# Perceiver block on one core: padded context tails, x by tiles, and another order at the end of the linear attention

## The chip, the cores and the metric

The kernel runs on one core of a Trainium2 chip. The metric is device microseconds (us) of one execution; lower is better. The time before the change is 684.81 us, the median of three runs (684.4 to 684.9).

The engines go by short names here. PE is TensorE (matmuls), PEld its weight loads, DVE is VectorE, ACT is ScalarE, POOL is GpSimd, and SP (SyncE) issues nearly all of the transfers. A float32 matmul stands in the trace as two instructions.

## What is computed

There are 8 sequences of 64 tokens, so 512 rows of x with 512 features, and for each sequence 1601 rows of context. Three residual blocks follow one another:

```python
x = x + _L0_xattn_ref(_layernorm(x), ctx_1024, W, b)
#   trans_q = ctx @ W.T + b; softmax(p @ trans_q.T); relu(att @ ctx @ W.T + b)
x = x + _L0_attn_ref(_layernorm(x), wq, wk, wv, wo, proj, ...)
#   h = ln(x); q, k = elu((h @ w) @ proj) + 1 per head; causal linear attention:
#   out_s = q_s . sum(k v) / (q_s . sum(k) + 1e-6); x + out @ wo; then a gelu MLP
x = x + _L0_ffn_ref(_layernorm(x), w_router, w0, w1, wo)
#   mixture of 8 experts, each token goes to 2 of them
```

The linear attention has 16 heads of 64 features. 512 = 4 tiles of 128 rows, and a tile holds two sequences.

## The kernel before

All is float32. The order of the instructions on every engine is the order in which the kernel's text issues them, SP included; nothing reorders them.

**Cross-attention.** The context comes twice: by key in `ctxT` tiles, for the scores, and by row in `ctx` tiles, for the weighted sum. `stream` lists these transfers and the later weights in one order; `issue_to` issues them from SP as buffers of a ring of 12 come free (a tile is about 1 MB at most, and PE frees one by finishing its matmuls). For each tile t of two sequences, `key_group` computes scores against a quarter of the keys, `softmax` follows, `turn_scores` transposes the weights, and `weigh(t, g)` multiplies them with 512 context rows of each of the two sequences. 1601 rows are 3 groups of 512 and 65 more. These 65 are the tail: `tail[t]` holds them for both sequences of the tile, 65 partitions with 2 x 512 numbers each (260 KB), in a buffer of its own (L188), and `weigh(t, 2)` adds its product (L482) to the sum that L472 has built up. The tail of tile t stands in the stream behind the third group of context rows of that tile.

**The start.** x is loaded in two transfers of two tiles each (L99), then W (`w_sb`), then the first key tiles. The statistics of x (L335), its normalization (L346) and transposes (L358) lead to the projection of x (L368), which PE does before the first scores.

**Linear attention.** The heads are taken in pairs, in 8 steps j = 0 to 7. A step has four parts:
- `linear(j, which)`: the projection of all 512 rows to q or k of the two heads, eight matmul instructions each (L595).
- `features(j)`: eight matmul instructions with `proj` (L611), then on DVE two minima (`ex`, L622), on ACT two exponentials (L623), on DVE `phi` of q and of k (L626).
- `products(j)`: q times k by tiles on PE (`qk`, L635), then masked on DVE (`masked`, L640).
- `attend_j(j)`: the denominator `den` (L652) and the numerator `num` (L662) on PE from `masked`, then on DVE `rden` (L670), its reciprocal (L671) and `a_t` (L672).

In the loop a step's parts stand between the projections of the next steps. The last parts have no projections to stand between: after the loop come `attend_j(6)`, `features(7)`, and then `output(t, js)`, the product of `a_t` with `wo` (L691) for tile t and the steps js, put between what is left. `output(0, ...)` and `output(1, ...)` need only steps up to 5 at first, and take 6 and 7 afterwards. Behind that come the residual sum and layer norm of each tile (`join`, `normal`, `turn_h2`), and the MLP.

**Mixture of experts.** Tokens are routed and gathered, and the experts' weights stream through the same ring. This is the longer half of the kernel, from about 400 us on.

Of the kernel before, what the change touches and what calls it, by code (L numbers as in the profile page):

```python
# [21 lines left out]
B, S, D = 8, 64, 512  # L22
LK = 1601
NT = B * S // P
KC = D // P
GK = 512
NG = LK // GK
TAIL = LK - NG * GK
SW = -(-LK // 4)
WIDTHS = [min(SW, LK - SW * g) for g in range(4)]  # L30
H, DH = 16, 64
# [15 lines left out]
def perceiver_kernel(  # L47
# [22 lines left out]
    nc = tc.nc  # L70
# [14 lines left out]
    def acc_bank(name):  # L85
        return ps.tile([P, 512], F32, tag="acc", name=name)
# [8 lines left out]


    xs = resid.tile([P, NT, D], F32, name="xs")
    for t in range(0, NT, 2):
        nc.sync.dma_start(xs[:, t : t + 2, :], x[:, t : t + 2, :])  # L99
    moe = ctx.enter_context(tc.tile_pool(name="moe", bufs=1))  # L100
    mid = ctx.enter_context(ExitStack())
    xinp = mid.enter_context(tc.tile_pool(name="xinp", bufs=1))
# [16 lines left out]
    def stream(key, src):  # L119
        order.append((key, src))  # L120

    def stream_keys(t, g):
        if t < NT:
            for h in range(2):
                src = context_t[2 * t + h, D * SW * g : D * (SW * g + WIDTHS[g])]
                stream(("ctxT", t, g, h), src.rearrange("(p c k) -> p c k", p=P, c=KC))
# [45 lines left out]
    def in_ring(key):  # L172
        return key[0] not in places_of and key not in places_of and key[0] != "tail"

    def issue_to(n):

        while issued[0] < min(n, len(order)):
            key, src = order[issued[0]]
            if in_ring(key) and len(held) >= RING:
                if held[0] not in freed:  # L180
                    return
                held.pop(0)
            if key in places_of:
                t_ = places_of[key]
                nc.sync.dma_start(t_, src)
            elif key[0] == "tail":
                t_ = tails.tile([P, 2, D], F32, tag="tail", name="_".join(str(k) for k in key))
                nc.sync.dma_start(t_[:TAIL, :, :], src)  # L188
            else:
                width = WIDTHS[key[2]] if key[0] == "ctxT" else 512  # L190
                t_ = ring.tile([P, 4, width], F32, tag="ring", name="_".join(str(k) for k in key))
                nc.sync.dma_start(t_, src)
                held.append(key)
            streamed[key] = t_
            issued[0] += 1
# [5 lines left out]
    def need(*key):  # L201
        if key[0] not in ("ctxT", "ctx", "tail", "wv"):
            done(*[k for k in held if place[k] < place[key] - AHEAD + 1])
            issue_to(place[key] + 1 + AHEAD)
        else:
            issue_to(len(order))
        return streamed[key]
# [156 lines left out]
    def pw_half(half, hc):  # L364
# [10 lines left out]
        nc.scalar.copy(pw_t[:, hc, cols], bank[:, : 2 * P])  # L375

    issue_to(len(order))
    turn_p(0)
    turn_p(1)
# [32 lines left out]
    def key_group(t, g):  # L412
# [8 lines left out]
        for c in range(KC):  # L421
# [9 lines left out]
        nc.scalar.activation(  # L431
            all_scores[t][:, g * SW : g * SW + width], sc[:, :width], AF.Identity, bias=pb[:, t : t + 1]
        )
# [11 lines left out]
    def turn_scores(t):  # L445
# [5 lines left out]
        for g in range(NG + 1):  # L451
# [6 lines left out]
            else:  # L458
                nc.tensor.transpose(bank[:TAIL, :P], scores[:, NG * GK : LK], ident)
                nc.scalar.copy(e_t[:TAIL, 4 * NG, :], bank[:TAIL, :P])  # L460

    all_av, all_xo = {}, {}

    def weigh(t, g):
# [15 lines left out]
        if g == NG - 1:  # L480
            for h in range(2):
                nc.tensor.matmul(  # L482
                    av[h * S : (h + 1) * S, :],
                    e_t[:TAIL, 4 * NG, h * S : (h + 1) * S],
                    need("tail", t)[:TAIL, h, :],
                    start=False,
# [96 lines left out]
    if True:  # L583
        a_t = la1.tile([P, H * DH // P, B * S], F32, name="a_t")

        nj = H * DH // P
# [18 lines left out]
        def features(j):  # L605

            pr = {which: acc_bank(f"pr_{which}_{j}") for which in ("wq", "wk")}
            for r in range(2):
                rows = slice(r * DH, (r + 1) * DH)
                for which, other in (("wq", r), ("wk", 1 - r)):  # L610
                    nc.tensor.matmul(  # L611
                        pr[which][other * DH : (other + 1) * DH, :],
                        proj2[rows, :],
                        lin[which, j][rows, :],
                        start=True,
                        stop=True,
                    )

            ex = {}
            for which in pr:  # L620
                ex[which] = la2.tile([P, B * S], F32, tag="ex", name=f"ex_{which}_{j}")
                nc.vector.tensor_scalar_min(ex[which], pr[which], 0.0)  # L622
                nc.scalar.activation(ex[which], ex[which], AF.Exp)  # L623
            for which in pr:
                phi[which, j] = la2.tile([P, B * S], F32, tag=f"phi_{which}", bufs=1, name=f"phi_{which}_{j}")
                nc.vector.scalar_tensor_tensor(phi[which, j], pr[which], 0.0, ex[which], ALU.max, ALU.add)  # L626

        def products(j):

            banks_ = [mm_bank(f"qk_{j}_{r}") for r in range(2)]  # L630
            for t in range(NT):
                cols = slice(t * P, (t + 1) * P)
                for r in range(2):
                    rows = slice(r * DH, (r + 1) * DH)
                    nc.tensor.matmul(  # L635
                        banks_[r][:, cols], phi["wk", j][rows, cols], phi["wq", j][rows, cols], start=True, stop=True
                    )
            for r in range(2):
                m = masked[j, r] = la2.tile([P, NT, P], F32, tag="masked", name=f"masked_{j}_{r}")
                nc.vector.tensor_tensor(  # L640
                    m,
                    banks_[r].rearrange("p (t q) -> p t q", t=NT),
                    mask[:, None, :].to_broadcast([P, NT, P]),
                    ALU.mult,
                )

        def attend_j(j):


            den = acc_bank(f"den_{j}")  # L650
            for r in range(2):
                nc.tensor.matmul(  # L652
                    den[r * DH : (r + 1) * DH, :],
                    ones[:, :DH],
                    masked[j, r].rearrange("p t q -> p (t q)"),
                    start=True,
                    stop=True,
                )
            num = acc_bank(f"num_{j}")
            for t in range(NT):  # L660
                for r in range(2):
                    nc.tensor.matmul(  # L662
                        num[r * DH : (r + 1) * DH, t * P : (t + 1) * P],
                        v_sb[:, t, (2 * j + r) * DH : (2 * j + r + 1) * DH],
                        masked[j, r][:, t, :],
                        start=True,
                        stop=True,
                    )
            rden = la2.tile([P, B * S], F32, tag="rden", bufs=1, name=f"rden_{j}")
            nc.vector.tensor_scalar_add(rden, den, 1e-6)  # L670
            nc.vector.reciprocal(rden, rden)  # L671
            nc.vector.tensor_tensor(a_t[:, j, :], num, rden, ALU.mult)  # L672
# [14 lines left out]
        def output(t, js):  # L687
            if t not in wo_banks:
                wo_banks[t] = (mm_bank if t < 2 else acc_bank)(f"wo_{t}")
            for j in js:  # L690
                nc.tensor.matmul(  # L691
                    wo_banks[t],
                    a_t[:, j, t * P : (t + 1) * P],
                    wo_r[j // 4][:, j % 4, :],
                    start=(j == 0),
                    stop=(j == nj - 1),
                )

        attend_j(nj - 2)
        features(nj - 1)  # L700

        warm2 = small.tile([P, 1], F32, tag="warm2", name="warm2")
        nc.scalar.activation(warm2, eps, AF.Sqrt)
        output(0, range(nj - 2))
        products(nj - 1)
        output(1, range(nj - 2))
        attend_j(nj - 1)
# [704 lines left out]
```

## Time and profile before

| | |
|---|---|
| median of the runs | 684.81 us |
| profiled execution, its own time | 685.44 us |
| its span, first to last instruction | 683.7 us |
| mean granted clock of TensorE | 0.983 |
| PE busy | 638.9 us (93%) |
| PEld busy | 296.2 us (43%) |
| DVE busy | 179.1 us (26%) |
| ACT busy | 128.2 us (19%) |
| moved by DMA | 138.04 MB, mean 202 GB/s |
| transfers of ctx / ctxT / tail | 24 of 1024 KB / 32 of about 800 KB / 4 of 260 KB |

A row of the timeline or of a group reads: start and duration in us, the engine, the kernel's line, the operation, output <- inputs, shapes, count; in brackets, the idle time before it and what ended that. The rows of 40 slices give busy time in tenths for equal parts of the span. A busy PE isn't PE at its peak, since the ends of matmuls are modelled. Idle time of an engine that is not the bound costs nothing.

### The profile page before, as it was taken

To read this page: it belongs to the slowest core of one execution; us is meant where nothing else is said; L and a number is where in the kernel's file an instruction comes from. 1 tells how busy PE (TensorE), PEld (TensorE's weight loads), DVE (VectorE), ACT (ScalarE), POOL (GpSimd) and SP (SyncE) were. 2 spreads that over 40 slices of the span, in tenths; PEclk is the share of its full clock that TensorE was granted. 3 is DMA by queue.
4 is the path that set the end of the run, shared out by engine and by line. 5 is a ranking of instruction groups with operands and counts; after the bars stand their busy time and mean duration, and the time that the engine had idled before them with its cause. 6 is when DMAs were issued, how large, how long until landed. Compare 5 with 4: busy or idle time off the path is not lost. (4 is left out here: it accounts for less than half of the span.)

```text
span 683.7 us, 6217 instructions
## 1 busy us (share of the span) xinstructions
PE 638.9 (93%) x2376; PEld 296.2 (43%) x2376; DVE 179.1 (26%) x403; ACT 128.2 (19%) x240; POOL 61.7 (9%) x81
## 2 busy tenths in 40 slices
PE   4998989799999999999999998898999999989993
PEld 3643434244444444445444455543444344434441
DVE  4011323132228687670000035310311101110100
ACT  2241223220132121122011200211111111111110
POOL 2000000000000000041000002331012202120000
PEclk9999999999999999999999999699999999999998
DMA  8999999999601103021311323127397595694711
GB/s 328 418 420 385 418 385 413 370 367 422 232 13 62 62 0 124 1 69 55 112 62 73 106 79 126 61 61 265 136 390 257 199 357 175 233 348 175 283 17 18
DMA packets 24222, 138.04 MB, mean 202 GB/s; under 512 B 4164, under 2 KB 4164, under 8 KB 11896
## 3 DMA queue, kind: packets, MB, share of 16 engines
q1 hardware_dynamic: 20056, 129.90, 49.0%
q0 software_dynamic: 3024, 6.58, 4.3%
q10 hardware_dynamic: 1104, 1.07, 0.4%
q8 instruction: 23, 0.38, 0.2%
q14 instruction: 15, 0.12, 0.1%
HBM read 132.56 MB, written 4.97 MB: 201 GB/s over the span
## 5 line engine op out<-in xcount | busy, mean ns | idle before, releaser
L1081 PE MATMUL up<-e_up,xgT 128*128 128x512 f32 x224 | 100.2, 595 | 1.2 <-PEq L1310 1.2
L1081 PEld LDWEIGHTS up<-e_up,xgT 128*128 128x128 f32 x224 | 40.9, 190 | 50.4 <-issue 50.4
L1089 PE MATMUL y<-e_wo,hidT 128*128 128x512 f32 x128 | 61.0, 599 | 0.0
L792 PE MATMUL mlp<-w,hid_sb 128*128 128x512 f32 x128 | 58.8, 597 | 0.0
L1046 DVE TENSOR_TENSOR mid<-up,act 128x256 f32<-128x256 f32 x35 | 14.9, 425 | 164.2 <-ACT act L1044 159.7
L771 PE MATMUL hid<-v_sb,w 128*128 128x512 f32 (+2 forms) x144 | 56.6, 545 | 0.0
L472 PE MATMUL av<-ctx,eT 128*64 128x512 f32 x192 | 48.4, 617 | 7.3 <-DMA ctx<-in_ctx_dram 6.5
L423 PE MATMUL sc<-ctxT,pw_t 128*64 128x401 f32 (+1 forms) x256 | 48.1, 501 | 0.7 <-DMA ctxT<-in_ctx_T_dram 0.7
L771 PEld LDWEIGHTS hid<-v_sb,w 128*128 128x128 f32 x144 | 26.2, 190 | 29.1 <-issue 27.3
L792 PEld LDWEIGHTS mlp<-w,hid_sb 128*128 128x128 f32 x128 | 23.4, 190 | 24.9 <-issue 24.9
L1044 ACT ACTIVATE act<-up 128x256 f32<-128x256 f32 x35 | 13.4, 383 | 104.5 <-PE up L1081 95.7
L786 POOL TENSOR_TENSOR xin<-xin,b_bc 128x512 f32<-128x512 f32 x4 | 5.1, 1263 | 295.3 <-DVE rstd_h L728 291.1
L423 PEld LDWEIGHTS sc<-ctxT,pw_t 128*64 128x64 f32 x256 | 20.3, 136 | 26.3 <-issue 22.9
L1062 POOL DMA_INDIRECT out_dram<-y_sb,dst_late x11 | 16.8, 1529 | 161.1 <-ACTq L1310 103.7
L1089 PEld LDWEIGHTS y<-e_wo,hidT 128*128 128x128 f32 x128 | 22.4, 190 | 19.5 <-issue 19.1
L595 PE MATMUL wk<-h_t,wk 128*128 128x512 f32 x64 | 29.5, 604 | 0.0
L595 PE MATMUL wq<-h_t,wq 128*128 128x512 f32 x64 | 29.4, 602 | 0.0
L532 PE MATMUL v<-wv,h_t 128*128 128x512 f32 x64 | 28.7, 597 | 0.6 <-DVE h_t L519 0.6
L472 PEld LDWEIGHTS av<-ctx,eT 128*64 128x64 f32 x192 | 13.9, 140 | 35.3 <-issue 24.6
L691 PE MATMUL wo<-wo,a_t 128*128 128x512 f32 x64 | 28.6, 597 | 0.0
L671 DVE RECIPROCAL rden<-rden 128x512 f32<-128x512 f32 x8 | 26.8, 3354 | 0.3
L828 DVE TENSOR_TENSOR xs<-mlp,xs 128x512 f32<-128x512 f32 x4 | 2.8, 692 | 87.3 <-PE mlp L792 87.3
(230 smaller groups left out, 653.1 us busy)
## 6 DMA issues: line engine op xcount, KB each, us to landing
e_up<-in_L_ffn_up_dram SPq DMA_DIRECT2D x32, 1024.0 KB, 7.9
ctx<-in_ctx_dram SPq DMA_DIRECT2D x24, 1024.0 KB, 17.4
ctxT<-in_ctx_T_dram SPq DMA_DIRECT2D x24, 802.0 KB, 15.7
e_wo<-in_L_ffn_wo_dram SPq DMA_DIRECT2D x16, 1024.0 KB, 10.0
w<-in_L_attn_w_dram SPq DMA_DIRECT2D x8, 1024.0 KB, 11.7
ctxT<-in_ctx_T_dram SPq DMA_DIRECT2D x8, 796.0 KB, 16.7
big_up<-in_L_ffn_up_dram SPq DMA_DIRECT2D x4, 1024.0 KB, 7.9
wv<-in_L_attn_wv_dram SPq DMA_DIRECT2D x2, 1024.0 KB, 13.0
```

What stands on the lines that cost most here:

```text
L423: nc.tensor.matmul(sc[h * S : (h + 1) * S, :width], pw_t[:, c, (2 * t + h) * S : (2 * t + h + 1) * S], keys[h][:, c, :], start=(c == 0), s ...
L472: nc.tensor.matmul(av[h * S : (h + 1) * S, :], e_t[:, 4 * g + j, h * S : (h + 1) * S], rows[h][:, j, :], start=(g == 0 and j == 0), stop=F ...
L532: nc.tensor.matmul(bank, h_t[:, c, t * P : (t + 1) * P], wv_n[:, c, :], start=(c == 0), stop=(c == KC - 1))
L595: nc.tensor.matmul(bank, w[:, c, (j % 4) * P : (j % 4 + 1) * P], h_t[:, c, :], start=(c == 0), stop=(c == KC - 1),)
L671: nc.vector.reciprocal(rden, rden)
L691: nc.tensor.matmul(wo_banks[t], a_t[:, j, t * P : (t + 1) * P], wo_r[j // 4][:, j % 4, :], start=(j == 0), stop=(j == nj - 1),)
L771: nc.tensor.matmul(hid_banks[f][:, tokens], w[:, c, (f % 4) * P : (f % 4 + 1) * P], h2_t[:, c, tokens], start=(c == 0), stop=(c == KC - 1),)
L792: nc.tensor.matmul(acc[t], hid[:, t * P : (t + 1) * P], need("w2", f // 4)[:, f % 4, :], start=(f == 0), stop=(f == FF // P - 1),)
L1046: nc.vector.tensor_tensor(hid, bank[:, FQ:], act, ALU.mult)
L1062: nc.gpsimd.indirect_dma_start(out=out, out_offset=bass.IndirectOffsetOnAxis(ap=dst[:n, :], axis=0), in_=y_sb[:n, :], in_offset=None, boun ...
L1081: nc.tensor.matmul(bank, xg_t[:, c, :], up_of[q][:, c, :], start=(c == 0), stop=(c == KC - 1))
L1089: nc.tensor.matmul(y, h_t[:, j, :], w[:, 2 * (q % 2) + j, :], start=(q + j == 0), stop=(q + j == NQ))
```

## The change

It has three parts.

The tails are padded on the host from 65 rows to 80, the next multiple of 16, and the transfer brings all 80; the matmuls read 65 of them as before. x is loaded in four transfers of one tile each in place of two of two tiles. And after the loop of the linear attention, `features(7)` is issued ahead of `attend_j(6)`, and `output(0, 0..5)`, which stood in one piece behind both, is cut in two: steps 0 to 2 go ahead of `attend_j(6)`, steps 3 to 5 behind it.

```diff
+TAIL_ROWS = -(-TAIL // 16) * 16
...
-    for t in range(0, NT, 2):
-        nc.sync.dma_start(xs[:, t : t + 2, :], x[:, t : t + 2, :])
+    for t in range(NT):
+        nc.sync.dma_start(xs[:, t, :], x[:, t, :])
...
-                nc.sync.dma_start(t_[:TAIL, :, :], src)
+                nc.sync.dma_start(t_[:TAIL_ROWS, :, :], src)
...
-        attend_j(nj - 2)
         features(nj - 1)
 
         warm2 = small.tile([P, 1], F32, tag="warm2", name="warm2")
         nc.scalar.activation(warm2, eps, AF.Sqrt)
-        output(0, range(nj - 2))
+        output(0, range(0, 3))
+        attend_j(nj - 2)
+        output(0, range(3, nj - 2))
         products(nj - 1)
         output(1, range(nj - 2))
         attend_j(nj - 1)
...
     tail = _np.asarray(inputs["ctx_1024"])[:, NG * GK :, :]
-    inputs["ctx_tail"] = tail.reshape(NT, 2, TAIL, D).transpose(0, 2, 1, 3)
+    tail = _np.pad(tail, ((0, 0), (0, TAIL_ROWS - TAIL), (0, 0)))
+    inputs["ctx_tail"] = tail.reshape(NT, 2, TAIL_ROWS, D).transpose(0, 2, 1, 3)
```

## The prediction

> **What bounds the kernel now.** I read the slices of the span first, then the timeline of PE by stage, then the windows around its stalls, then the rows at the place of the edit. The slices (each 17.1 us):
>
> ```profile
> PE   4998989799999999999999998898999999989993
> ...
> PEclk9999999999999999999999999699999999999998
> DMA  8999999999601103021311323127397595694711
> ```
>
> PE is busy in nearly every slice. DMA is full in the first ten (to 171 us) and in no later one; there alone can a transfer set the pace. The clock's one digit below 9 inside the span stands for 427 to 444 us. In that first part PE waits long three times, each time for context rows:
>
> ```profile
> 61.92 4.92 PE L472 MATMUL av<-ctx,eT 128*64 128x512 f32 x13 [2.29 <-DMA ctx<-in_ctx_dram]
> ...
> 94.77 3.22 PE L472 MATMUL av<-ctx,eT 128*64 128x512 f32 x13 [1.47 <-DMA ctx<-in_ctx_dram]
> ...
> 129.58 3.22 PE L472 MATMUL av<-ctx,eT 128*64 128x512 f32 x13 [2.73 <-DMA ctx<-in_ctx_dram]
> ```
>
> After 129.58 no PE wait in this stage is for a transfer, so the landing before it sets the stage's end; PE time saved ahead of it is given back as longer waits. The stalls lie beside the tails. Windows (us, PE, PEld, DVE, ACT, POOL, clock, DMA share, GB/s):
>
> ```profile
> 44.00:58.00 14.00, 14.00 (x77) 5.98 (x76) 0.00 (x0) 2.86 (x6) 0.00 (x0) 1.00 1.02 420
> 58.00:63.00 5.00, 2.71 (x12) 0.83 (x11) 1.82 (x1) 2.20 (x3) 0.00 (x0) 0.98 1.02 301
> 63.00:90.50 27.50, 27.50 (x131) 11.74 (x129) 7.43 (x17) 5.48 (x12) 0.00 (x0) 0.94 1.02 420
> ...
> 125.00:130.50 5.50, 1.97 (x9) 0.54 (x10) 1.82 (x1) 3.60 (x4) 0.00 (x0) 1.00 1.02 276
> ```
>
> The stream runs at 420 GB/s and falls to 301 while the first tail's packets are under way; likewise to 299 (90.5 to 95.5), 276, and 268 (147.5 to 153.5). The engines stay busy (share 1.02): every packet takes longer. Beyond the tail's own bytes a dip loses 119*5/420 = 1.42 us of stream, then 1.44, 1.89 and 2.17.
>
> From 171 us on PE is the bound. The end of the linear attention on PE, then on DVE:
>
> ```profile
> 266.85 1.16 PE L635 MATMUL qk<-phi_wq,phi_wk 64*128 64x128 f32 x16
> 269.62 1.24 PE L652 MATMUL den<-masked,ones 128*64 128x512 f32 x3 [1.62 <-DVE masked L640]
> ...
> 273.12 5.42 PE L691 MATMUL wo<-wo,a_t 128*128 128x512 f32 x12
> 278.91 1.16 PE L635 MATMUL qk<-phi_wq,phi_wk 64*128 64x128 f32 x16 [0.37 <-DVE phi_wk L626]
> 280.00 5.42 PE L691 MATMUL wo<-wo,a_t 128*128 128x512 f32 x12
> 285.35 1.08 PE L652 MATMUL den<-masked,ones 128*64 128x512 f32 x4
> ```
>
> ```profile
> 264.82 3.35 DVE L671 RECIPROCAL rden<-rden 128x512 f32<-128x512 f32 x1
> ...
> 268.89 1.28 DVE L640 TENSOR_TENSOR masked<-qk,mask 128x512 f32<-128x512 f32 x2
> ...
> 272.06 3.35 DVE L671 RECIPROCAL rden<-rden 128x512 f32<-128x512 f32 x1
> ...
> 276.12 0.68 DVE L622 TENSOR_SCALAR ex_wq<-pr_wq 128x512 f32<-128x512 f32 x1
> ```
>
> PE finishes qk of step 6 near 267.9 but has to wait for masked, which stands on DVE behind step 5's reciprocal; then features 7's chain stands behind step 6's reciprocal, and qk of step 7 waits.
>
> **The order of the last steps.** Nothing is added or removed; features(7) moves ahead of attend_j(6), with half of output(0) between them. PE now takes 285.35 - 266.85 = 18.50 us from qk of step 6 to den of step 7. The same blocks without a wait, from starts of rows: qk 1.09 (278.91 to 280.00); features 1.02 (its first matmul is at 272.10, wo at 273.12); twelve wo matmuls 5.35 (280.00 to 285.35), of which 12*0.43 is spacing and 0.2 the switch to another kind, so six take 2.58 + 0.2 = 2.78; den and num 1.88 (285.35 to 287.23). The new order costs 1.09 + 1.02 + 2.78 + 1.88 + 2.78 + 1.09 + 5.35 = 15.99: **2.51 us less**. From the waits: 1.68 ahead of den, 0.60 inside that block (269.62 to 272.10 in place of 1.88) and 0.44 ahead of qk, less 0.2 for one switch more.
>
> Is it covered? Counting on the old clock, features end at 268.95, wo at 271.7, and masked is ready at 270.2: 1.5 us of cover. On DVE features 7 then follow masked at once: two minima, two phi at some 0.6 each with an exponential between them, as at 250.20 to 252.93, ready near 272.9; qk needs them at 276.4. DVE goes on with rden 6 (den ready at 272.8), its reciprocal (3.35) and a_t 6 to 277.7; masked 7 ends near 279.0, and attend 7 asks for it at 282.8. Queued behind the moved work are thus a_t 6 (read by wo after attend 7) and masked 7, both over 3 us early. Banks: features 7 take those of features 6, read by 264.2; attend 6 takes those of step 5, free at 268.97. ACT's exponentials come earlier, its table load stays behind them. No DMA is issued here, so no queue is passed. What is late next is a_t 7, as now: wo of step 7 waits 0.47 for it at 291.4, and all shifts together.
>
> Behind that, weight transfers wait for ring slots that PE frees and shift with it (no PE wait for a weight tile in the trace), so the gain reaches the end. One thing can bend it: from 428.1 to 441.7 the clock is at half in four steps of 3.41 us. A step more or less costs PE up to 1.7 us; which way a shift of 2.5 us turns it the trace can't say. I take 0 and keep 1.7 both ways.
>
> **x in four transfers.** Two issues more on SP, 0.4 us each (the two take 0.81 to 1.68), ahead of w_sb; 1 MB is then queued at 2.5 us, over 2 us of stream, so nothing runs dry. The first tile lands half a transfer earlier (512 KB at 420 GB/s are 1.25 us, so some 0.6), and its statistics start near 4.2 instead of 4.84. PE starts at most 0.6 earlier and gives it back at 61.92. Packets of 2 KB take 0.084 us where those of 4 KB take 0.159: 512*0.084 against 256*0.159 over 16 engines is 0.14 us of stream. SP lets eight transfers be open; two small ones ahead alter that only at the start. Taken at 0, between 0.6 less and 0.2 more.
>
> **Tails of 80 rows.** What is added is 15*4 KB per tail, 61 KB, 0.15 us at 420 GB/s; what may go is the dip. A tail's completion count rises in 14 steps where a transfer of 128 rows takes 16, so at most 14 engines carry its 65 packets, the busiest five or more. If 80 rows fill all 16, the busiest still carries five, and the first 65 rows stay where they are. The bounds: all that lies ahead of 129.5 of the dips vanishes, 1.42 + 1.44 + 1.5 = 4.4 us less (PE's three waits, 6.5 in all, can give that); or the dips grow with the rows, by 80/65, some 0.35 each, and the bytes 0.15: 2.8*0.5 = 1.4 more. Nearest row: x itself came in packets of 4 KB over 128 rows at 418 GB/s (4.5 to 5.0 us), so packet size isn't the cause, and covering 80 rows is nearer to 65 than to 128. I take 0.
>
> [...] No run here shows a tail of another height.
>
> **The sum.** 2.51 less + 0 + 0: the profiled execution, 685.44 (span 683.7), goes to 682.9. It lies 0.63 above the median of the runs, 684.81, so the forecast is 682.3.
>
> **The rivals.** *The dips go* (0.2): engines in step and no short engines' lead; for it, the dips grow from tail to tail (1.42 to 2.17) as the landings spread; against it, that the rows stay. Then 4.4 less besides: about 677.9. *The dips grow with the rows* (0.1): 1.4 back: about 683.7. *Slower* (0.08): three more engines, writing rows beyond 64 as well, draw the other transfers deeper into the slow-down, and the rate in a window falls from 300 to 200 GB/s: its 5*300 = 1500 KB then take 7.5 us, 2.5 more, 2.8 times ahead of 129.5 (the third tail's window lies ahead of it with 0.8), so 684.8 + 7.0 - 2.5 = 689.3. It decides from a rate below 234: 1500/234 is 1.4 us more per tail, 3.9 in all, the 2.5 given back and 1.4 more; for it speaks that in the dips packets of all engines, also those with other rows, take 1.5 to 2 times as long; against it, that the trace has so low a rate in one place alone, 181 GB/s at 12.5 to 13.0 us, beside the transfer of `xb_bc`. *The order doesn't pay* (0.07): DVE takes another order, or PE's waits move to phi 7; that leaves 684.8; the counted slack of 1.5 and 3.5 us speaks against it.
>
> **How the numbers follow.** The main case has 0.55, 682.3 with its own range 680.6 to 684.0 (the clock's 1.7 each way). The low end reaches to the case without dips, 678.0; the high end takes in the growth of the dips, 684.4. A measurement of this kernel tells about 0.2% (1.4 us) from no change: faster is under 683.4, 0.51 of the main case's 0.55, the 0.2 without dips and 0.05 of the third, 0.76; same 0.15; slower 0.09, the fourth case and a hundredth.
>
> **What would show it.** Right: den of step 6 with no wait for masked, qk of step 7 with none for phi, den of step 7 some 18.5 - 2.5 us after qk of step 6; the rate beside tails still near 300, ctx rows of the third pair landing near 129.5. Wrong: a rate near 420 beside the tails (far faster), or near 200 (slower); a new PE wait for a_t; more than four half-clock steps near 430.

## The result and the profile after

The changed kernel takes 686.38 us, the median of 14 runs (682.55 to 688.6); beside them the kernel before took 684.96 (14 runs, 684.4 to 686.98). The ratio is 1.001 [0.9998, 1.0023]: no gain, and within the 0.2% that the prediction called the same. The forecast was 682.3 with a range of 678.0 to 684.4. The profiled execution is the longest of the runs, 688.6 (span 686.9); a second one took 685.05, and where the two differ in what matters below, it is said.

The slices, to be held against those of before:

```profile
PE   4998989799999999999999999798999999989993
PEclk9998999999999999999999999699999999999998
DMA  8999999999420202011212223227497595694711
```

What was lost, was lost by 171 us: part of the transfers that came in the eleventh slice now come in the twelfth (4 and 2 where there were 6 and 0), and PE's clock has a second digit below 9, in the fourth slice (51 to 69 us). The linear attention itself did as forecast. PE's timeline there:

```profile
272.19 1.16 PE L636 MATMUL qk<-phi_wq,phi_wk 64*128 64x128 f32 x16
...
274.30 2.84 PE L692 MATMUL wo<-wo,a_t 128*128 128x512 f32 x6
277.08 1.08 PE L653 MATMUL den<-masked,ones 128*64 128x512 f32 x4
277.99 1.04 PE L663 MATMUL num<-masked,v_sb 128*64 128x128 f32 x16
278.96 2.84 PE L692 MATMUL wo<-wo,a_t 128*128 128x512 f32 x6
281.73 1.16 PE L636 MATMUL qk<-phi_wq,phi_wk 64*128 64x128 f32 x16
282.82 5.42 PE L692 MATMUL wo<-wo,a_t 128*128 128x512 f32 x12
288.17 1.08 PE L653 MATMUL den<-masked,ones 128*64 128x512 f32 x4
```

From qk of step 6 to den of step 7 it is 288.17 - 272.19 = 15.98 us. No bracket is left: neither den nor qk waits. But qk of step 6 starts at 272.19, where it was 266.85, so 5.3 us were lost before this place (3.3 in the second profile, 270.14).

Two places show where. First the start. Each row of a window gives its bounds and length, then PE, PEld, DVE, ACT and POOL, then clock, DMA share and GB/s. Before:

```profile
3.50:5.00 1.50, 0.00 (x0) 0.00 (x0) 0.16 (x1) 0.00 (x0) 1.28 (x8) 1.00 0.93 333
5.00:6.50 1.50, 0.00 (x0) 0.00 (x0) 1.43 (x5) 0.29 (x1) 0.75 (x1) 1.00 1.10 431
```

After:

```profile
3.50:5.00 1.50, 0.00 (x0) 0.00 (x0) 0.73 (x2) 0.00 (x0) 1.28 (x8) 1.00 0.91 224
5.00:6.50 1.50, 0.00 (x0) 0.00 (x0) 1.27 (x5) 0.54 (x2) 0.75 (x1) 1.00 0.97 244
```

DVE begins earlier, as forecast, but the bytes come at 224 and 244 GB/s where they came at 333 and 431. By the last packets of each transfer, x is complete at 8.81 (6.49 before) and `w_sb` at 11.33 (8.98 before), 2.35 us late; SP's wait for the first key tile behind it ends at 13.31 where it ended at 11.11. In the second profile `w_sb` is complete at 9.81. PE's rows of the first projection and of the three long waits:

```profile
11.46 5.25 PE L369 MATMUL pw<-h_t,w_sb 128*128 128x256 f32 x16 [2.00 <-DMA w_sb<-in_L_xattn_W_dram]
...
63.39 2.83 PE L473 MATMUL av<-ctx,eT 128*64 128x512 f32 x6 [2.60 <-DMA ctx<-in_ctx_dram]
...
98.19 2.37 PE L473 MATMUL av<-ctx,eT 128*64 128x512 f32 x10 [2.23 <-DMA ctx<-in_ctx_dram]
...
133.23 3.73 PE L473 MATMUL av<-ctx,eT 128*64 128x512 f32 x10 [2.71 <-DMA ctx<-in_ctx_dram]
```

The wait for `w_sb` is new. The third long wait ends at 133.23 where it ended at 129.58 (at 129.91 in the second profile). Second, the windows of tail and clock in the profile after:

```profile
44.00:58.00 14.00, 13.76 (x75) 6.57 (x75) 0.00 (x0) 2.86 (x6) 0.00 (x0) 1.00 1.02 419
58.00:65.00 7.00, 4.05 (x14) 1.04 (x12) 1.82 (x1) 2.32 (x3) 0.00 (x0) 0.82 1.02 300
...
62.00:70.00 8.00, 6.61 (x18) 2.01 (x20) 0.00 (x0) 1.64 (x2) 0.00 (x0) 0.57 1.02 384
134.00:138.00 4.00, 4.00 (x14) 1.13 (x11) 0.00 (x0) 0.00 (x0) 0.00 (x0) 0.57 1.01 418
```

The dip beside the first tail is there as before: 300 GB/s against 419. Stream time lost beside the four tails, from packets, is 2.00, 2.17, 2.82 and 1.64 us (before, worked out alike: 1.41, 1.51, 2.22, 2.21). Of the third, some 0.8 us was lost from 118 to 124 us, ahead of that tail's packets (128.2 to 133.3). What has grown is the half clock at the end of the waits: from 62.4 to 69.2 (before: 62.8 to 66.2) and from 134.1 to 137.5 (before: not at all). In the second profile it is at half from 129.1 to 135.9 alone. The steps are 3.41 us each, with a granted clock of 0.50, and in them matmul instructions of 512 columns start 0.85 us apart, at the full clock 0.43: half the work, so 1.7 us less in a step.

### The profile page after: what moved, and what is told of

It reads as the page before. It is cut to its first block, busy times and chain, and to the rows that moved or that the text cites. A ratio compares the mean times of both kernels' runs of the same rounds, so it can differ in the third digit from the quotient of the medians.

```text
span 686.9 us, 6217 instructions
## 1 busy us (share of the span) xinstructions
PE 641.2 (93%) x2376; PEld 296.7 (43%) x2376; DVE 179.7 (26%) x403; ACT 128.2 (19%) x240; POOL 61.4 (9%) x81
## 5 line engine op out<-in xcount | busy, mean ns | idle before, releaser
L473 PE MATMUL av<-ctx,eT 128*64 128x512 f32 x192 | 51.9, 649 | 9.0 <-DMA ctx<-in_ctx_dram 9.0
L473 PEld LDWEIGHTS av<-ctx,eT 128*64 128x64 f32 x192 | 15.4, 146 | 39.0 <-issue 25.7
```

Of the source, the lines that this page charges most:

```text
L473: nc.tensor.matmul(av[h * S : (h + 1) * S, :], e_t[:, 4 * g + j, h * S : (h + 1) * S], rows[h][:, j, :], start=(g == 0 and j == 0), stop=F ...
```

## The experiments

Ratios are to the kernel before, run beside each, with a 95% interval; 0.1% is 0.69 us.

**The three parts alone, and the order with tails of 128 rows.** Before: 685.49.

The order alone:

```diff
-        attend_j(nj - 2)
         features(nj - 1)
...
-        output(0, range(nj - 2))
+        output(0, range(0, 3))
+        attend_j(nj - 2)
+        output(0, range(3, nj - 2))
```

> The kernel before with the new order of the last steps alone. Theory A (the prediction's: the order gains 2.5 us, x and the tails cost nothing) and theory B (the order gains 2.5, and x and the tails give it back in the transfer-bound first stage) both expect 2.5 us less than before, 682.4, and 15.99 us from qk of step 6 to den of step 7 in the profile. Rival C (the order's gain does not reach the end, as routing or the clock take it back) expects within 0.7 us of before with the same 15.99 us in place.

683.68 us, ratio 0.9971 [0.9960, 0.9981], so 2.0 us less (1.3 to 2.7): the order pays, and the 2.5 that its rows say lie within the interval.

x in four alone:

```diff
-    for t in range(0, NT, 2):
-        nc.sync.dma_start(xs[:, t : t + 2, :], x[:, t : t + 2, :])
+    for t in range(NT):
+        nc.sync.dma_start(xs[:, t, :], x[:, t, :])
```

> The kernel before with x in four transfers alone. Theory A expects no difference (within 0.5 us), the wait ahead of the third pair of context rows taking up what the start gains or loses. Theory B expects 1 to 2.4 us more, w_sb landing near 11 us instead of 8.98, and the context rows of the third pair landing that much behind 129.5. Rival C: no difference.

688.16 us, 1.0039 [1.0024, 1.0054]: 2.7 us more, for an edit taken at nothing. The second half of x is where it slows; `w_sb` is complete at 11.23:

```profile
3.50:5.00 1.50, 0.00 (x0) 0.00 (x0) 0.74 (x2) 0.00 (x0) 1.28 (x8) 1.00 0.60 150
```

At 150 GB/s the 16 engines are busy 60% of the time only, though `w_sb` is already queued behind. This is the lowest of the profiles: five others with x in four like this have 224 to 268 GB/s there, at a share of 0.76 to 0.91.

Tails of 80 rows alone:

```diff
+TAIL_ROWS = 80
...
-                nc.sync.dma_start(t_[:TAIL, :, :], src)
+                nc.sync.dma_start(t_[:TAIL_ROWS, :, :], src)
```

> The kernel before with tails of 80 rows alone. Theory A expects no difference (within 0.5 us) and rates beside the tails near 300 GB/s as before. Theory B expects 1 to 1.4 us more, the windows of low rate growing by 80/65 in length or depth. That the missing engines caused the low rate would give some 4 us less and 420 GB/s beside the tails.

686.10 us, 1.0007 [0.9997, 1.0016]: 0.5 us more, or nothing. The three together, -2.0 + 2.7 + 0.5 = 1.2, agree with the whole change's +0.7 (-0.1 to +1.6).

The new order with tails padded to a whole tile, and x in two transfers as before:

```diff
+TAIL_ROWS = 128
```

> The new order, and tails of 128 rows (63 of them zeros), with x in two transfers. Three readings of the low rate beside the tails: if it comes from a transfer that covers only part of the 128 partitions, 128 rows show 420 GB/s throughout; a tail then costs 0.6 us for 252 KB more and saves 1.4 to 2.2, net some 2 us less ahead of the third pair, so 680 with the order's 2.5. If it comes from the number of packets of 4 KB, the low rate lasts twice as long and the time is some 4 us above e1_order. If a tail's cost is bytes alone, 1.7 us above e1_order.

678.92 us, 0.9901 [0.9886, 0.9916], 4.8 us less than the order alone: the best version of all, ahead of both kernels, though each tail moves nearly twice the bytes. The windows beside its first and third tail, and its clock at the place of the third wait:

```profile
57.00:62.00 5.00, 3.64 (x19) 1.42 (x17) 1.82 (x1) 1.66 (x2) 0.00 (x0) 1.00 1.02 416
...
122.00:128.00 6.00, 3.83 (x18) 1.01 (x16) 1.82 (x1) 3.60 (x4) 0.00 (x0) 1.00 1.02 419
```

The dip is gone: 0.05, 0.06, 0.10 and 0.03 us of stream lost. PE's waits shrink, and the stage ends earlier (the first projection of the linear attention starts at 180.4, with the order alone at 184.7):

```profile
60.49 3.22 PE L473 MATMUL av<-ctx,eT 128*64 128x512 f32 x13 [1.36 <-DMA ctx<-in_ctx_dram]
...
92.36 3.22 PE L473 MATMUL av<-ctx,eT 128*64 128x512 f32 x13 [0.80 <-DMA ctx<-in_ctx_dram]
...
125.76 3.22 PE L473 MATMUL av<-ctx,eT 128*64 128x512 f32 x13 [1.35 <-DMA ctx<-in_ctx_dram]
```

Its profile has no half clock before 421 us, where that of the order alone has one step (129.0 to 132.4). How much of the 4.8 us is the stream and how much the clock wasn't measured apart.

**Which heights keep the dip.** Before: 686.28. Both have the new order and x in two transfers. One brings 64 of the tail's 65 rows:

```diff
+TAIL_ROWS = 64
...
-                    e_t[:TAIL, 4 * NG, h * S : (h + 1) * S],
-                    need("tail", t)[:TAIL, h, :],
+                    e_t[:TAIL_ROWS, 4 * NG, h * S : (h + 1) * S],
+                    need("tail", t)[:TAIL_ROWS, h, :],
```

The other pads them to 112:

```diff
+TAIL_ROWS = 112
```

> The new order, and tails of 64 rows: the last key of each sequence is left out of the weighted sum, so the time alone is to be read. 64 rows are four packets for each of 16 engines. If low rates come from covering half of the partitions, they stay near 300 GB/s beside the tails and the time is within 0.7 us of e1_order (683.7). If they come from five packets per engine, or from a row count that is no power of two, they go, and the time is some 4 us below e1_order, 679 to 680.

> The new order, and tails of 112 rows (7 packets on each of 16 engines). If the low rate shrinks as more of the partitions are covered, the loss beside a tail lies between those of 80 rows (1.4 us and more) and of 128 (none): 680 to 682. If only a full 128 rows avoid it, the loss is as with 80 rows or more, some 1 us above e1_order.

The packets on each engine in the two expectations are an estimate, rows over 16; no record tells the engines apart. 64 rows: 686.25, 0.9999 [0.9989, 1.0008]. 112 rows: 686.05, 0.9997 [0.9988, 1.0007]. Both are about 2 us worse than the order with 65 rows, more than either expectation had. Their profiles have half clock behind the waits from 95.0 to 101.8 and 132.5 to 135.9 (64 rows) and from 128.4 to 135.2 (112), one or two steps more than the order alone, which may be the 2 us; no run separates it. The windows of 64 rows:

```profile
58.00:63.00 5.00, 3.26 (x16) 1.04 (x14) 1.82 (x1) 2.17 (x3) 0.00 (x0) 1.00 1.03 307
92.00:97.00 5.00, 2.11 (x6) 0.53 (x6) 1.82 (x1) 3.60 (x4) 0.00 (x0) 0.79 0.97 257
```

and of 112:

```profile
92.00:97.00 5.00, 2.82 (x12) 0.77 (x12) 1.82 (x1) 3.60 (x4) 0.00 (x0) 1.00 1.01 308
126.00:132.00 6.00, 2.58 (x6) 0.72 (x8) 1.82 (x1) 3.13 (x4) 0.00 (x0) 0.70 1.01 272
```

So the loss isn't in proportion to the rows left out. 112 rows have 343 GB/s beside the first tail and lose 0.96, 1.74, 2.38 and 2.44 us beside the four tails, much like 65 or 80, and 128 rows lose none. A loss that shrinks with the rows missing is refuted; why only the full height escapes isn't settled (see the last section).

**How x is cut.** In the same comparison, four transfers from a tensor laid out tile by tile on the host (256 KB in one piece each):

```diff
-    for t in range(0, NT, 2):
-        nc.sync.dma_start(xs[:, t : t + 2, :], x[:, t : t + 2, :])
+    for t in range(NT):
+        nc.sync.dma_start(xs[:, t, :], x[t])
```

> Four transfers of x as in e2_x4, but x laid out tile by tile, so that each transfer reads 256 KB that lie together instead of 2 KB out of every 8 KB. If the loss of e2_x4 (2.7 us) comes from reading with that step, it goes: within 0.7 us of before, w_sb landing near 9 us. If it comes from packets of 2 KB or from two issues more, it stays: 2 to 2.7 us above before, w_sb near 11.

and x in one transfer:

```diff
-    for t in range(0, NT, 2):
-        nc.sync.dma_start(xs[:, t : t + 2, :], x[:, t : t + 2, :])
+    nc.sync.dma_start(xs, x)
```

> x in one transfer of 8 KB rows, one issue fewer than before. If the start of the transfers sets the first stage, larger pieces gain a little, 0 to 1 us, w_sb landing near 8.5, though the first statistics start at 5.5 to 6 us instead of 4.84. If PE's start sets it, 0.5 to 1 us more.

Tile by tile: 687.00, 1.0012 [1.0003, 1.0022]. One transfer: 685.83, 1.0001 [0.9989, 1.0012]. Tile by tile, 0.8 us (0.2 to 1.5) of the 2.7 are left, so most of the cost goes with the 2 KB pieces that lie 8 KB apart, and the rest with four transfers as such. The same windows of the start, tile by tile:

```profile
3.50:5.00 1.50, 0.00 (x0) 0.00 (x0) 1.43 (x3) 0.29 (x1) 1.28 (x8) 1.00 0.91 259
5.00:6.50 1.50, 0.32 (x2) 0.35 (x3) 1.43 (x5) 0.29 (x1) 0.76 (x1) 1.00 1.17 440
```

and in one transfer:

```profile
3.50:5.00 1.50, 0.00 (x0) 0.00 (x0) 0.00 (x0) 0.00 (x0) 1.28 (x8) 1.00 0.98 410
5.00:6.50 1.50, 0.00 (x0) 0.00 (x0) 0.66 (x1) 0.00 (x0) 0.77 (x1) 1.00 1.01 421
```

One transfer has `w_sb` complete at 8.31, earlier than before (8.98), and gains nothing: its first statistics start later (5.84), and the stage's end is set elsewhere. Tile by tile, all of x is there at 6.15, earlier than before (6.49), yet `w_sb` only at 10.26 and not near 9. SP issues `w_sb` at 1.27 with one transfer of x, at 1.74 with two and at 2.69 with four: in these three profiles the landing shifts with the issue and by more than it, so about half of the 2.35 us of the change seems to come from the two issues more.

Then, before: 685.95, four transfers again, with x padded so that the pieces of 2 KB lie 10 KB apart:

```diff
-        nc.sync.dma_start(xs[:, t : t + 2, :], x[:, t : t + 2, :])
+        nc.sync.dma_start(xs[:, t, :], x[:, t, :])
...
+    inputs["x"] = _np.pad(x_rows, ((0, 0), (0, 1), (0, 0)))
```

> Four transfers of x as in e2_x4, with x padded in memory so that the 2 KB pieces lie 10 KB apart instead of 8 KB. If the power-of-two step is what makes their reading slow, most of the loss goes, as in e5_x4_together: within 1 us of before, all of x landed by 6.5 us. If any scattered pieces of 2 KB are slow, it stays: 2 to 2.7 us above before, the last tile of x landing near 8.8 us and w_sb near 11.

687.22, 1.0024 [1.0013, 1.0035], x complete at 7.55 and `w_sb` at 10.15. The time lies between that of the pieces 8 KB apart and that of tile by tile, with intervals that overlap both ways. How much of the cost is the distance of the pieces and how much their size isn't settled.

**x with the dips gone.** In the same comparison, the order and 128 rows with x in one and in four transfers:

> The new order, tails of 128 rows, x in one transfer. With the low rates gone the first stage still waits for transfers (PE waited 1.9, 1.4 and 1.9 us in e4_order_tail128), so a landing of w_sb earlier by 0.7 us, as in e6_x1, may come through whole: 678.2, or nothing if the slower engine of the sixteen sets the landing: 678.9.

> As e4_order_tail128, with x in four transfers as in the change. If the late start of the stream passes through the transfer-bound stage to the end, 2 to 2.7 us above e4_order_tail128: 681 to 681.6. If it cost time only by making the low rates beside the tails worse, nothing: 678.9.

679.51, 0.9909 [0.9890, 0.9928], and 678.89, 0.9913 [0.9890, 0.9937]. With x in two it was 0.9901 [0.9886, 0.9916]. Here x in four costs no 2.7 us that can be seen, though in its profile the first projection of the linear attention still starts 1.5 us later (181.9 against 180.4). The intervals reach 1.3 and 1.6 us to either side, so about that much may be hidden. Neither profile has half clock before 421 us. (PE's waits with x in two were 1.36, 0.80 and 1.35 us by the rows above, shorter than the first expectation has them.)

**What the late stream does to the clock.** The parts alone left this open: with x in four the third wait ends at 130.02, only 0.4 us after before's, yet the linear attention starts 3.1 us later (187.4 against 184.3). Between them lies a half clock that before's profile doesn't have. The row behind the wait shows it: 5.93 us for 13 matmuls that took 3.22 before.

```profile
130.02 5.93 PE L472 MATMUL av<-ctx,eT 128*64 128x512 f32 x13 [2.65 <-DMA ctx<-in_ctx_dram]
```

Windows of 15 us around that wait; before:

```profile
125.00:140.00 15.00, 11.46 (x38) 4.50 (x38) 3.33 (x4) 4.18 (x5) 0.00 (x0) 1.00 1.02 369
```

x in four alone:

```profile
125.00:140.00 15.00, 11.57 (x31) 3.57 (x28) 2.57 (x2) 3.60 (x4) 0.00 (x0) 0.77 1.02 379
```

PE is busy as long (11.57 against 11.46), but with 31 matmuls in the records instead of 38. To test it, three matmuls whose result is never read go ahead of the third group of context rows of tiles 0 to 2, where PE would wait; into the change, into x in four, and into the kernel before (before: 686.18):

```diff
+        if g == NG - 1 and t < 3:
+            idle = mm_bank(f"idle_{t}")
+            for c in range(3):
+                nc.tensor.matmul(idle, pw_t[:, c, :P], pw_t[:, c, :], start=(c == 0), stop=(c == 2))
```

> The changed kernel with three idle matmuls (2.6 us, result unused) on PE ahead of the third context group of tiles 0 to 2, where it waits 2.8 to 3.4 us for rows. They fit into the wait. Theory D (much of the loss is PE running at half clock for 3.4 to 6.8 us after a wait of over 2.5 us) expects no half-clock stretch between 60 and 140 us and 1.5 to 3 us less than the change, 683.4 to 685. Theory B (the loss is the later landing of rows alone) expects no gain: 686.4 or up to 1 us more.

> e2_x4 with the same idle matmuls. Theory D: 1.5 to 3.4 us less than e2_x4 (its profile has two half-clock stretches behind the third wait), 685 to 686.5, so that x in four transfers costs about 1 us of late stream. Theory B: as e2_x4, 688.

> The kernel before with the same idle matmuls. Its profile has a half-clock stretch at 62.8 only, ahead of a later wait, so theory D expects 0 to 1 us less (runs of before that fall into a stretch near 130 gain), theory B 0 to 0.5 more.

The change with it: 683.60, 0.9967 [0.9954, 0.9980], 2.8 us below the change without. x in four: 685.43, 1.0005 [0.9992, 1.0017] (without: 1.0039). The kernel before: 684.11, 0.9982 [0.9969, 0.9996], so it had some of this loss itself. In the change's timeline the idle work fills the wait:

```profile
126.55 2.84 PE L474 MATMUL idle<-pw_t 128*128 128x512 f32 x6
129.33 1.07 PE L477 MATMUL av<-ctx,eT 128*64 128x512 f32 x2
131.30 3.22 PE L477 MATMUL av<-ctx,eT 128*64 128x512 f32 x13 [0.90 <-DMA ctx<-in_ctx_dram]
```

The window of 15 us around it has the full clock:

```profile
125.00:140.00 15.00, 14.10 (x49) 5.23 (x46) 2.66 (x3) 4.12 (x5) 0.00 (x0) 1.00 1.02 374
```

In none of the three is the clock at half anywhere before 426 us. So the half clock behind the waits is shown to cost, and keeping PE busy takes it away.

**When the clock falls.** The late stream isn't needed for it: the order alone, with x in two, has a step at half from 129.0 to 132.4 too. In each of the 17 profiles kept, all changes of the clock are whole multiples of 3.41 us apart, on a grid that lies elsewhere in each. Cut by that grid, the profiles have 3194 windows at full clock. PE was busy for at most 1.51 us in 49 of them, and after each of these the next window was at half; with 1.52 or 1.53 us it was so after two of four, and with 1.57 or more after none. A window at half was followed by full clock only where PE was busy for 3.02 us or more of it. So it is not a wait's length alone that decides, but how it falls on the grid. The longest wait of the kernel before, 2.73 us ahead of 129.58, is cut by it into two windows with 1.78 and 1.52 us of work, and costs no half clock; the change's, 2.71 us, leaves one window of 0.86 us (130.68 to 134.09).

## Why the prediction was wrong

The forecast gain didn't come: two steps failed, and a third was on the mark.

- **The order of the last steps: right.** 15.99 us were forecast for the stretch and 15.98 are there, without the waits that were to go. Alone it brought 2.0 (1.3 to 2.7) of the 2.51, and the stage behind it kept the gain: from the first projection of the linear attention to the first of the MLP it is 308.6 - 189.6 = 119.0 us, before 305.8 - 184.3 = 121.5. The rival "the order doesn't pay" is refuted.
- **x in four transfers: the step that failed.** It was taken at 0, at most 0.2 more, from "512*0.084 against 256*0.159" and "nothing runs dry". The sum takes the engines to be full. It measured +2.7 alone (1.6 to 3.7): the engines fell to a share of 0.60 and 150 GB/s with work still queued (0.91 and 224 GB/s in the change's profile), and about half of the delay of `w_sb` seems to come from the two issues that "nothing runs dry" was to cover. The earlier start of the statistics (forecast near 4.2) did come, and was worth nothing, since the projection then waited 2.00 us for `w_sb`, which the prediction had behind it in the queue but did not follow.
- **The clock: the step that was missing.** The prediction kept 1.7 us both ways for the half clock near 430 alone. The row that it showed for 63 to 90.5, with a clock of 0.94, already held a half step behind the first wait, and it was read past. Later transfers lengthen PE's waits for context rows (9.0 us in all where it was 6.5; 7.6 in the second profile), and behind some of them PE runs at half for one or two steps of 3.41 us. Behind the third wait nothing gives that back. With the waits filled, the change stands at 0.9967 and the kernel before at 0.9982, so 1.0 us better; without, 0.7 worse. By these medians the half clock costs the change 1.7 us more than it costs the kernel before, but each of the three ratios has an interval of about 0.9 us to either side. x in four then costs 1.6 still (1.0005 against 0.9982). That fits the late stream: in the profiles with the waits filled, the linear attention starts at 184.96 with x in four and at 182.93 without.
- **Tails of 80 rows: right, with half the reason.** Taken at 0 and measured at +0.5 (-0.2 to +1.1), inside its bounds of -4.4 and +1.4. "The dips go" did not come with 80 rows, and "covering 80 rows is nearer to 65 than to 128" held. But nearness is the wrong idea: 112 rows are no better (308 and 272 GB/s in the windows above, against 416 and 419 with 128). The price named for that rival was nearly the truth for 128 rows: 4.8 measured, 4.4 forecast, in part by luck if some of the 4.8 is the clock's.
- **The slower rival: refuted as a mechanism.** It had dips deepened by the rows beyond 64, with a rate below 234 GB/s and 7.0 us to pay. With 80 rows alone the four tails lose 1.64, 1.83, 2.26 and 2.30 us of stream, before 1.41, 1.51, 2.22 and 2.21: 0.7 us more in all. That isn't clear of the scatter: from 3 us ahead of a tail's first packet to 3 us behind its last, the eight profiles with 65 rows lose 6.1 to 8.0 us at their four tails, the four with 80 rows 6.9 to 7.9. No 5 us of the profiles with 80 rows have less than 243 GB/s, where the case needs under 234. Whether the dips grow with the rows at all (1.4 more was the price) isn't settled. No run shows its three engines more, nor the short engines' lead of the rival "the dips go": what the traces show is a completion count that rises in 14 steps with 65 rows, one of them 0.5 us after the issue and ahead of the first packet (45.15 against 57.77 at the first tail), and in 16 with 80, with dips in both. And packets in the dips took 1.1 to 1.6 times as long in the median (last section), not 1.5 to 2, with no record of which engine carried them.

PE needn't be idle through a whole stretch of 3.41 us for the clock to fall: none of the three waits in the changed kernel is longer than 2.71 us in one piece, and windows with up to 1.51 us of work were followed by half clock here. Ahead of the wait of 2.71 stands a burst of 1.04 us and another wait of 1.08, so that PE worked 1.04 us in 4.83. Waits of 1.36, 0.80 and 1.35 us, with 128 rows, brought no half clock.

## What to carry to other kernels

Where a full stream of transfers sets the pace, look at the rate beside each odd-shaped transfer: filling it to 128 partitions, at nearly twice its bytes, was worth 4.8 us of 684 here, and each smaller height that was tried (64, 80, 112) was worth nothing. Don't cut the first load of a stream into pieces of half the size for an earlier start unless what follows it in the queue can be late: alone it cost 2.7 us here. And a wait of PE cost more than its length where the clock fell behind it (13 matmuls took 5.93 us in place of 3.22): cover it, with idle matmuls if need be (2.8 us less for the change), or count the half clock in the sum. In the profiles here it fell after each of the 49 stretches of 3.41 us in which PE worked 1.51 us or less, and after none with 1.57 or more.

## What was not expected of the hardware

- Beside a first tail of 64, 65, 80 or 112 partitions the stream ran at 307, 301, 300 and 343 GB/s in the windows above, beside one of 128 at 416. The packets of the other transfers were slower too: in the profile before, those of 8 KB took 0.31 us in the median away from the tails, and 0.34, 0.38, 0.47 and 0.51 between the first and the last packet of the four of them. Not every one was: at the first tail a quarter took 0.32 or less. Why stays open. No record here shows which engine writes which row.
- With x in four transfers of 2 KB pieces that lie 8 KB apart the rate was 150 GB/s from 3.5 to 5.0 us (224 to 268 in five other profiles), with the whole 8 KB in one transfer 410.
- The clock differs between executions of one and the same kernel, and the time with it: of the 100 executions of the kernel before that were run beside the experiments, the 38 with a mean clock of 0.980 took 686.4 us on average and the 15 with 0.984 took 684.6. The difference is about that of one half-clock step.
